# A stack of four gated cross-attention and FFN layers on one core: the first Mamba preparation kept on chip, and input weights kept for a layer's products

## The chip, the cores and the metric

The kernel is one program on one core of a Trainium2 chip. Its time is the device time of one execution in microseconds (us); where several executions were timed, the median stands. Engines: PE multiplies matrices (PEld loads its stationary operand), DVE, ACT and POOL work on tiles of 128 partitions, and SP issues most DMA transfers. ACT issues some too.

## The reference, cut to what matters

Four layers, each a gated cross-attention block and a gated FFN, act on x of shape (4, 512, 512), with a context ctx of shape (4, 512, 256):

```python
x = x + tanh(g_xattn[0]) * L0_xattn(ctx, layernorm(x), ...)   # Mamba
x = x + tanh(g_ffn[0])   * L0_ffn(layernorm(x), ...)          # gated, 2 of 4 kept
x = x + tanh(g_xattn[1]) * L1_xattn(layernorm(x), ctx, ...)   # attention over channels
x = x + tanh(g_ffn[1])   * L1_ffn(layernorm(x), ...)          # ternary weights
x = x + tanh(g_xattn[2]) * L2_xattn(ctx, layernorm(x), ...)   # Mamba
x = x + tanh(g_ffn[2])   * L2_ffn(layernorm(x), ...)          # fp8 weights
x = x + tanh(g_xattn[3]) * L3_xattn(layernorm(x), ctx, ...)   # 16-head attention
x = x + tanh(g_ffn[3])   * L3_ffn(layernorm(x), ...)          # quantised both sides
```

The Mamba blocks are what the change touches. Their recurrence depends on ctx alone; z, made of x, only multiplies its result:

```python
x = einsum('bld,ed->bel', ctx, in_proj_w)
u = silu(conv1d(x, conv_w, width 4, causal) + conv_b)
dt_low, B, C = split(einsum('bdl,ed->bel', u, x_proj_w))      # 16, 16 and 16 rows
dt = softplus(einsum('brl,dr->bdl', dt_low, dt_proj_w) + dt_proj_b)
state = state * exp(dt * A) + (dt * u) * B                    # for each of 512 times
y = sum over 16 states of state * C
y = (y + D * u) * silu(z)
```

## The kernel before, in words

A batch is a "head" (l, b): l is 0 for the first Mamba block and 1 for the second, b one of four batches. The heads run in the order (0,0), (0,1), (1,0), (0,2), (1,1), (0,3), (1,2), (1,3). An l = 0 head goes through Mamba, l0f (the first FFN), l1attn and l1x, and l1f; an l = 1 head through Mamba, l2f and l3x; the last FFN, l3f, comes behind.

For each head the Mamba work has three parts. `mamba_in` (L462) multiplies ctx with the input weights: 4 tiles of 128 channels by 512 times, each from 2 x 3 products, since operands are split into a high and a low part. `mamba_pre` (L486) makes u (convolution L500, tanh L504, L505), the product xd with B, C and dt's low rows (L529), the product dtp (L546 for the first head, L566 for others), softplus through a polynomial log1p (ACT squares L483, DVE steps L484), and from dt also du = dt * u and y = D * u. The scan does 64 steps, 16 states by 4 channel tiles. A step (`state`, L599) is an exp on ACT (L602), a product with B on POOL (L603), the scan on DVE (L605) and a product with C (L606); the sum over states is on POOL (L624), or for the first head on PE (L644).

The first head's three parts, the prologue, run ahead of everything in the pool `pp`; its preparation keeps u, dt, du and y in SBUF (`if pp`). Among its scan steps the loop at the end of the kernel calls `mamba_in` for the seven other heads, whose results go to DRAM (dxin). Their preparations and scans are side work (lists `pres` and `side`): generators that `tick` draws on between the pieces of the main path, the first preparation at once in the first l0f tile (`finish(whole)`). They pass everything through DRAM: u, dtp (ddtp), dt and du (dst) and y (dy) are written and read again, by `copy` (SP queue, L254) and `keep` (ACT queue, L259). B and C go to DRAM as dbc, and each state's two rows are loaded as a bc tile broadcast to all partitions (L596).

`unit` (L266) loads a weight or ctx: at its first use raw, then split on ACT (high part, L263) and on DVE or POOL (low part, L264) and written to DRAM; later uses load the split form (L278). All l0f and l1f weights pass this way in the first head.

The main path needs a scan's end in `xmamba`: the stored y is loaded, multiplied with silu(z) (L663, L665), transposed on PE (xm, L669) and added to x (L671). For the next l = 0 head this is called inside the present block's last `down`.

A scheduler fixes each engine's order when the program is built. It lists the instructions by priority, which is program order; `tick` raises the number for side work, `copy` for its transfers (by 200 in the first block, 60 later), so that these stand behind. At run time each engine and each DMA queue works in its fixed order. Tiles come from pools with a number of buffers per tag, and an instruction that takes a buffer waits for the last reader of the one before.

Of the kernel before, what the change touches and what calls it, by code (L numbers as in the profile page):

```python
# [10 lines left out]
F32 = mybir.dt.float32  # L11
# [9 lines left out]
ADD, SUB, MUL = ALU.add, ALU.subtract, ALU.mult  # L21

B, S, D, CD = 4, 512, 512, 256
# [53 lines left out]
def tile_flamingo(ctx: ExitStack, tc: tile.TileContext, I, out):  # L77
    nc = tc.nc
    v, s, g, pe, sy = nc.vector, nc.scalar, nc.gpsimd, nc.tensor, nc.sync
# [58 lines left out]
    side, pres, prep = [], [], []  # L138
# [73 lines left out]
    for l in range(2):  # L212
        o = l * PAR_MW
        a = cp.tile([128, 64], F32, name=f"nA{l}")
# [3 lines left out]
        c = cp.tile([128, 20], F32, name=f"cw{l}")  # L218
# [24 lines left out]
    scr = {}  # L243
    turn = {"split": 0, "w": 0}

    def dram(key, shape, dt):
        t = dr.tile(shape, dt, name=nm("d" + key), tag=nm("d"))
        return t

    def copy(dst, src):  # L250

        behind = COPIES if phase[0] > 0 else COPIES_FIRST
        tc.cur_priority += behind
        sy.dma_start(dst, src)  # L254
        tc.cur_priority -= behind

    def keep(dst, src):

        s.dma_start(dst, src)  # L259
# [3 lines left out]
        s.copy(dst[:, 0], src)  # L263
        (lo_eng or v).tensor_tensor(dst[:, 1], src, dst[:, 0], op=SUB)  # L264

    def unit(kind, i, cols=512, p=None, tag="w"):  # L266

        t = T(p or wp, [128, 2, cols], FR, tag)
        key = (kind, i)
        if key not in scr:  # L270
            raw = T(wrp, [128, 512], F32, "wr")
            sy.dma_start(raw[:, :cols], I[kind][i])
            turn["split"] += 1
            split(t, raw[:, :cols], lo_eng=g if turn["split"] % 2 or phase[0] < 0 else v)
            scr[key] = dram(kind, [128, 2 * cols], F32)
            copy(scr[key], t.rearrange("p a c -> p (a c)").bitcast(F32))
        else:
            sy.dma_start(t.rearrange("p a c -> p (a c)").bitcast(F32), scr[key])  # L278
        return t
# [177 lines left out]

    xin = {}

    def mamba_in(l, b, stay=None):  # L460

        cu = [unit("ctxT", 2 * b + k) for k in range(2)]  # L462
        iw = [unit(f"M{l}_in", k) for k in range(2)]
        for d in range(4):
            ps = stay() if stay else mmps("in")
            c = slice(d * 128, d * 128 + 128)
            for k in range(2):
                mm3(ps, iw[k][:, 0, c], iw[k][:, 1, c], cu[k][:, 0], cu[k][:, 1], k == 0, k == 1)
# [14 lines left out]
            s.activation(q, t, AF.Square, bias=lpb[:, i : i + 1])  # L483
            v.scalar_tensor_tensor(ac, q, LP[i][1], t if i == 0 else ac, op0=ADD, op1=MUL)  # L484

    def mamba_pre(l, b, mp, pp=None):  # L486

        M = lambda tag, shape=(128, 512), dt=F32: T(mp, list(shape), dt, tag)
        po = l * PAR_MW
        ud = []  # L490
# [31 lines left out]
        for d in range(4):  # L522
# [5 lines left out]
            c = slice(d * 80, d * 80 + 80)  # L528
# [7 lines left out]
        bcd = dram("bc", [32, 512], F32)  # L536
# [27 lines left out]
        for d in range(4):  # L564
            ps = mbps("dtp")
            pe.matmul(ps, dw[:80, 0, d * 128 : d * 128 + 128], st[:80], start=True, stop=True)  # L566
            x = M("mt")
            s.activation(x, ps, AF.Identity, bias=dtb(d))
            keep(tmp[:, d], x)
        yield 1.0  # L570
        for d in range(4):
            dt = M("mt")
            copy(dt, tmp[:, d])
            t = M("mt")
            s.activation(t, dt, AF.Abs)
            s.activation(t, t, AF.Exp, scale=-1.0)
            s.activation(dt, dt, AF.Relu)
            ac = M("mt")
            log1p(t, ac, mbps)
            v.scalar_tensor_tensor(dt, ac, LP_K, dt, op0=MUL, op1=ADD)  # L580
            r = [dram("st", [128, 512], F32) for i in range(2)]
            copy(r[0], dt)
            u = M("mt")
            copy(u, ud[d])
            g.tensor_tensor(dt, dt, u, op=MUL)
            copy(r[1], dt)
            g.tensor_scalar(u, u, Dc(d), 0.0, op0=MUL, op1=ADD)
            copy(ysc[l, b][d], u)
            sc.append(r)
            yield 3.4  # L590
        mst[l, b] = bcd, sc

    def bc_tile(bcd, n, p, bufs, queue=sy):

        bc = p.tile([128, 2, 512], F32, tag="bc", name=nm("bc"), bufs=bufs)
        queue.dma_start(bc, bcd.rearrange("(c n) l -> n c l", c=2)[n].partition_broadcast(128))  # L596
        return bc

    def state(l, b, n, d, dt, du, bc, db, last=v):  # L599
# [8 lines left out]
    def mamba_scan(l, b, mp, red):  # L608

        M = lambda tag: T(mp, [128, 512], F32, tag)  # L610
        bcd, sc = mst[l, b]
        dts, us, ys = [], [], []
        for d in range(4):
            for tag, r, src in (("dt", dts, sc[d][0]), ("du", us, sc[d][1]), ("y", ys, ysc[l, b][d])):
                x = M(tag)
                copy(x, src)
                r.append(x)
        ahead = bc_tile(bcd, 0, mp, mbufs["bc"])
        for n in range(NST):
# [785 lines left out]
    mctx = ExitStack()  # L1405
    wrp = mctx.enter_context(tc.tile_pool(name="wr", bufs=4))
    mp = mctx.enter_context(tc.tile_pool(name="m", bufs=4))
    mbufs = {"bc": 2, "mt": 4, "db": 3, "fc": 2, "fw": 2, "kn": 4, "fv": 4, "sq": 1}
    _T = T

    def T(p, shape, dt, tag, name=None):
# [33 lines left out]
    heads = [Head(*h) for h in ((0, 0), (0, 1), (1, 0), (0, 2), (1, 1), (0, 3), (1, 2), (1, 3))]  # L1445
    with psum(mb=2, y=4), tc.tile_pool(name="pro", bufs=1) as pp:
        z4 = lambda: pp.tile([128, 512], F32, tag="z", name=nm("z"), bufs=8)
        mamba_in(0, 0, lambda: bank("y", "in"))
        list(mamba_pre(0, 0, mp, pp))
        scan = mamba_scan_pe(0, 0, pp)  # L1450
        for i, _ in enumerate(scan):
            if i % 7 == 6 and i < 49:
                h = heads[i // 7 + 1]
                mamba_in(h.l, h.b)
            if i == 32:
                heads[0].load(z4, z4)
        for h in heads[1:]:
            side.append(((h.l, h.b), mamba_scan(h.l, h.b, mp, on_g)))
            pres.append(((h.l, h.b, "pre"), mamba_pre(h.l, h.b, mp)))
        xmamba(0, 0, heads[0].xs, heads[0].zs, None, mbps)  # L1460
        heads[0].turn(mbps)
    side.append((("w3",), l3f_prep(mp)))
# [113 lines left out]
```

## Time and profile before

| What | us |
|---|---|
| Median of 3 timed runs | 3509.45 |
| Lowest, highest | 3498.4, 3509.68 |
| The profiled execution | 3500.79 |
| Its span, first to last instruction | 3499.0 |
| PE busy in the span | 3063.6 (88%) |
| DVE busy | 2536.3 (72%) |
| ACT busy | 1988.9 (57%) |
| POOL busy | 1728.6 (49%) |
| Moved by DMA | 720.95 MB, 206 GB/s in the mean |

Milestones of the profiled execution, from the rows of the tiles named:

| Milestone | from, us | to, us |
|---|---|---|
| scan of head (0,0) (L605, db00x) | 59.6 | 193.1 |
| its x update (L671) | 199 | 203 |
| first l0f, gate and up (L700 to L703) | 223 | 341 |
| dtp product of head (0,1) (L566) | 255 | 261 |
| scan of head (0,1) (db01x) | 358.2 | 619.3 |
| l1f of head (0,0), gate and up | 465 | 535 |
| l1f of head (0,0), down (L416) | 549 | 589 |
| x update of head (0,1) | 637 | 641 |
| second l0f, gate and up | 657 | 796 |
| scan of head (1,0) (db10x) | 670.6 | 976.8 |
| scan of head (0,2) (db02x) | 1013.7 | 1270.4 |

Read it so: busy shares over the whole span mix stages with different limits. A stage is read from its own stretch, by who is busy in it and what the others wait for. The granted clock of PE was 0.946 in the mean.

### The profile page before, as it was taken

To read this page: it belongs to the slowest core of one execution; us is meant where nothing else is said; L and a number is where in the kernel's file an instruction comes from. 1 tells how busy PE (TensorE), PEld (TensorE's weight loads), DVE (VectorE), ACT (ScalarE), POOL (GpSimd) and SP (SyncE) were. 2 spreads that over 40 slices of the span, in tenths; PEclk is the share of its full clock that TensorE was granted. 3 is DMA by queue.
4 is the path that set the end of the run, shared out by engine and by line. 5 is a ranking of instruction groups with operands and counts; after the bars stand their busy time and mean duration, and the time that the engine had idled before them with its cause. 6 is when DMAs were issued, how large, how long until landed. Compare 5 with 4: busy or idle time off the path is not lost.

```text
span 3499.0 us, 41084 instructions
## 1 busy us (share of the span) xinstructions
PE 3063.6 (88%) x12460; PEld 1994.9 (57%) x12474; DVE 2536.3 (72%) x4160; ACT 1988.9 (57%) x4405; POOL 1728.6 (49%) x1369
## 2 busy tenths in 40 slices
PE   6779986588898889888998899899998999989996
PEld 4347463464666555475575555475766555666663
DVE  6867897899779789889688799975335445655454
ACT  6437474454654777654564577553534767656673
POOL 5823795347667578556576689820101313213121
PEclk8889998799999899999999899999999999999998
DMA  8649577875685565485677554397755444466551
GB/s 308 211 169 357 196 264 269 309 250 186 229 275 176 205 195 143 132 298 186 203 260 240 178 169 159 93 340 258 247 194 186 133 121 157 151 211 206 177 157 46
DMA packets 323070, 720.95 MB, mean 206 GB/s; under 512 B 33025, under 2 KB 34433, under 8 KB 322849
## 3 DMA queue, kind: packets, MB, share of 16 engines
q1 hardware_dynamic: 269008, 617.65, 51.7%
q10 hardware_dynamic: 53840, 100.68, 10.1%
q8 instruction: 99, 1.62, 0.2%
q14 instruction: 123, 1.00, 0.1%
HBM read 553.25 MB, written 164.95 MB: 205 GB/s over the span
## 4 chain that ended last, share of the span: by engine, by line
PE 38%; DVE 24%; ACT 9%; DMA 9%; issue 8%; POOL 7%; SPq 0%; ACTq 0%; DVEq 0%; POOLq 0%
DVE mb L605 7%; PE acc L416 3%; POOL y L624 3%; PE S L833 3%; PE down L1029 2%; PE gate L700 2%; PE gate L701 2%; PE up L700 2%; PE up L701 2%; PE l L1373 2%; PE po L1011 2%; ACT P L840 1%; PE down L1163 1%; PE pT L848 1%; PE acc L895 1%
## 5 line engine op out<-in xcount | busy, mean ns | idle before, releaser
L602 ACT ACTIVATE mb<-dt,nA 128x512 f32<-128x512 f32 x512 | 352.3, 692 | 452.4 <-DVE db10x L606 64.6
L340 POOL TENSOR_TENSOR sm<-sm,mhalf 128x4 f32<-128x4 f32 (+4 forms) x104 | 143.5, 1380 | 516.2 <-DVE sm L370 233.8
L700 PE MATMUL gate<-xT,w 128*128 128x512 f32 x624 | 257.9, 413 | 46.1 <-DVE xT L264 20.1
L833 PE MATMUL S<-k,q 128*128 128x512 f32 x512 | 263.1, 626 | 28.8 <-ACT P L840 23.7
L700 PE MATMUL up<-xT,w 128*128 128x512 f32 x624 | 246.8, 396 | 8.5 <-DVE hf L753 5.5
L701 PE MATMUL gate<-xT,w 128*128 128x512 f32 x624 | 250.6, 402 | 0.0
L416 PE MATMUL acc<-w,hf 128*128 128x512 f32 x512 | 229.5, 604 | 22.6 <-DVE hf L728 17.1
L834 DVE TENSOR_REDUCE st<-S 128x1 f32<-128x512 f32 x256 | 173.4, 682 | 99.3 <-PE S L833 98.6
L701 PE MATMUL up<-xT,w 128*128 128x512 f32 x624 | 244.8, 392 | 0.0
L340 POOL TENSOR_TENSOR sml<-sml,mhalf 128x1 f32<-128x1 f32 x32 | 17.8, 558 | 418.7 <-DVE sml L370 223.5
L840 ACT ACTIVATE P<-S,st,sm 128x512 f32<-128x512 f32 x256 | 199.5, 784 | 39.3 <-DVE st L838 28.9
L1011 PE MATMUL po<-pt,v 128*128 128x512 f32 x384 | 203.9, 614 | 19.6 <-ACT pt L850 19.6
L848 PEld LDWEIGHTS pT<-ident,P 128*128 128x128 f32 x1024 | 127.3, 144 | 128.7 <-issue 56.8
L850 ACT COPY pt<-pT 128x512 f32<-128x512 f32 x256 | 148.8, 590 | 77.7 <-PE pT L848 75.4
L848 PE MATMUL pT<-ident,P 128*128 128x128 f32 x1024 | 164.7, 281 | 29.6 <-ACT P L840 12.1
L416 PEld LDWEIGHTS acc<-w,hf 128*128 128x128 f32 x512 | 97.7, 193 | 146.1 <-issue 112.9
L703 PE MATMUL gate<-xT,w 128*128 128x512 f32 x432 | 172.7, 400 | 0.0
L1029 PE MATMUL down<-wo,h 128*128 128x512 f32 x384 | 170.7, 593 | 0.0
L703 PE MATMUL up<-xT,w 128*128 128x512 f32 x432 | 169.7, 393 | 0.0
L700 PEld LDWEIGHTS gate<-xT,w 128*128 128x128 f32 x624 | 121.4, 195 | 81.7 <-DVE xT L264 21.6
L343 PE MATMUL Q<-w,xT 128*128 128x256 f32 x512 | 159.4, 312 | 7.3 <-ACT xT L263 5.2
L416 PE MATMUL acc<-w,h 128*128 128x512 f32 x352 | 154.0, 594 | 0.0
(314 smaller groups left out, 9110.0 us busy)
## 6 DMA issues: line engine op xcount, KB each, us to landing
bc<-dbc ACTq DMA_DIRECT2D x105, 512.0 KB, 5.5
w<-dL_g SPq DMA_DIRECT2D x81, 512.0 KB, 5.3
w<-dL_u SPq DMA_DIRECT2D x81, 512.0 KB, 5.1
w<-in_L_d_dram SPq DMA_DIRECT2D x68, 512.0 KB, 5.8
w<-dL_q SPq DMA_DIRECT2D x64, 512.0 KB, 5.0
w<-dL_gu SPq DMA_DIRECT2D x48, 512.0 KB, 5.1
v<-dv SPq DMA_DIRECT2D x80, 256.0 KB, 5.6
k<-dk SPq DMA_DIRECT2D x80, 256.0 KB, 3.6
```

What stands on the lines that cost most here:

```text
L416: pe.matmul(ps, h[:, c], w, start=first, stop=last)
L602: s.activation(ps, dt, AF.Exp, scale=nA[l][:, d * 16 + n : d * 16 + n + 1])
L605: v.tensor_tensor_scan(h, ps, db, 0.0, MUL, ADD)
L700: pe.matmul(ps, wh[:, c], xT[k][:, 0], start=k == 0, stop=False)
L701: pe.matmul(ps, wh[:, c], xT[k][:, 1], start=False, stop=wl is None and k == 3)
L703: pe.matmul(ps, wl[:, c], xT[k][:, 0], start=False, stop=k == 3)
L833: pe.matmul(ps, q[:, c], k[t * len(k) // NT], start=True, stop=True)
L834: v.tensor_reduce(st[:, t : t + 1], ps, AX.X, ALU.max, negate=True)
L840: s.activation(p, ps, AF.Exp, scale=r, bias=m, accum_out=st[:, 8 + t : 9 + t])
L848: pe.transpose(ps[:, t * 128 : t * 128 + 128], pt[t][:, kt * 128 : kt * 128 + 128], ident)
L1011: pe.matmul(po, vs[kt][:, c], u, start=kt == 0, stop=kt == 3)
L1029: pe.matmul(ps, hs[j][:, c], ws[j // 2][:, j % 2], start=j == 0, stop=j == 3)
```

## The change

Four things are changed.

1. `unit` takes `again`; with `again=False` a first use isn't written to DRAM. The input weights of a layer are loaded and split once, into the tag "iw" (2 buffers) of the prologue's pool, and kept in `inw` for the layer's four products, instead of being stored and loaded again for each head.
2. The seven `mamba_in` calls among the scan's steps go by layer and batch, (0,1), (0,2), (0,3), (1,0) to (1,3), instead of in the order of the heads.
3. Everything that they issue on SP stands behind the issue of the fourth bc tile (`rows[3]`): `tc.issue_after` orders instructions of the same engine, without a semaphore.
4. The preparation of head (0,1), the first that runs beside the main path, is called with `here=True`: dtp goes straight into the dt tile, log1p and softplus work on it there, u is loaded from DRAM into the du tile, y and du are made there, and `mamba_scan` takes the three tiles of each d as they are. The first three reloads of u for xd and the dxin and u transfers stay.

```diff
-    def unit(kind, i, cols=512, p=None, tag="w"):
+    def unit(kind, i, cols=512, p=None, tag="w", again=True):
...
-            scr[key] = dram(kind, [128, 2 * cols], F32)
-            copy(scr[key], t.rearrange("p a c -> p (a c)").bitcast(F32))
+            if again:
+                scr[key] = dram(kind, [128, 2 * cols], F32)
+                copy(scr[key], t.rearrange("p a c -> p (a c)").bitcast(F32))
...
-    def mamba_in(l, b, stay=None):
+    def mamba_in(l, b, pp, stay=None):
...
-        iw = [unit(f"M{l}_in", k) for k in range(2)]
+        if l not in inw:
+            inw[l] = [unit(f"M{l}_in", k, p=pp, tag="iw", again=False) for k in range(2)]
+        iw = inw[l]
...
-            x = M("mt")
+            x = M("dt" if here else "mt")
             s.activation(x, ps, AF.Identity, bias=dtb(d))
-            keep(tmp[:, d], x)
+            if here:
+                sc.append([x])
+            else:
+                keep(tmp[:, d], x)
...
-            dt = M("mt")
-            copy(dt, tmp[:, d])
+            if here:
+                dt = sc[d][0]
+            else:
+                dt = M("mt")
+                copy(dt, tmp[:, d])
...
+            if here:
+                du, y = M("du"), M("y")
+                sy.dma_start(du, ud[d])
+                g.tensor_scalar(y, du, Dc(d), 0.0, op0=MUL, op1=ADD)
+                g.tensor_tensor(du, dt, du, op=MUL)
+                sc[d] += [du, y]
+                yield 3.4
+                continue
...
-        queue.dma_start(bc, bcd.rearrange("(c n) l -> n c l", c=2)[n].partition_broadcast(128))
+        i = queue.dma_start(bc, bcd.rearrange("(c n) l -> n c l", c=2)[n].partition_broadcast(128))
+        rows.append(i.ins)
...
-        dts, us, ys = [], [], []
-        for d in range(4):
+        dts, us, ys = zip(*sc) if len(sc[0]) == 3 else ([], [], [])
+        for d in range(4 - len(dts)):
...
-        mamba_in(0, 0, lambda: bank("y", "in"))
+        mamba_in(0, 0, pp, lambda: bank("y", "in"))
...
-                h = heads[i // 7 + 1]
-                mamba_in(h.l, h.b)
+                with tc.issue_after(rows[3]):
+                    mamba_in(*divmod(i // 7 + 1, B), pp)
...
-            pres.append(((h.l, h.b, "pre"), mamba_pre(h.l, h.b, mp)))
+            pres.append(((h.l, h.b, "pre"), mamba_pre(h.l, h.b, mp, here=h is heads[1])))
```

More of the change, by code (lines that the diff above doesn't have):

```diff
@@ L458, in tile_flamingo @@
     xin = {}
-    def mamba_in(l, b, stay=None):
+    inw = {}
+    def mamba_in(l, b, pp, stay=None):
         cu = [unit("ctxT", 2 * b + k) for k in range(2)]
-        iw = [unit(f"M{l}_in", k) for k in range(2)]
+        if l not in inw:
+            inw[l] = [unit(f"M{l}_in", k, p=pp, tag="iw", again=False) for k in range(2)]
+        iw = inw[l]
         for d in range(4):
@@ L484, in log1p, with mamba_pre @@
             v.scalar_tensor_tensor(ac, q, LP[i][1], t if i == 0 else ac, op0=ADD, op1=MUL)
-    def mamba_pre(l, b, mp, pp=None):
+    def mamba_pre(l, b, mp, pp=None, here=False):
         M = lambda tag, shape=(128, 512), dt=F32: T(mp, list(shape), dt, tag)
@@ L591, in mamba_pre @@
         mst[l, b] = bcd, sc
+    rows = []
     def bc_tile(bcd, n, p, bufs, queue=sy):
         bc = p.tile([128, 2, 512], F32, tag="bc", name=nm("bc"), bufs=bufs)
-        queue.dma_start(bc, bcd.rearrange("(c n) l -> n c l", c=2)[n].partition_broadcast(128))
+        i = queue.dma_start(bc, bcd.rearrange("(c n) l -> n c l", c=2)[n].partition_broadcast(128))
+        rows.append(i.ins)
         return bc
@@ L1407, in tile_flamingo @@
     mp = mctx.enter_context(tc.tile_pool(name="m", bufs=4))
-    mbufs = {"bc": 2, "mt": 4, "db": 3, "fc": 2, "fw": 2, "kn": 4, "fv": 4, "sq": 1}
+    mbufs = {"iw": 2, "bc": 2, "mt": 4, "db": 3, "fc": 2, "fw": 2, "kn": 4, "fv": 4, "sq": 1}
     _T = T
```

## The prediction, made before the changed kernel had run

> **What bounds the kernel now.** I read the page's slices first, then the busy time by stretch, then who waited for whom, and last the rows of the tiles that the change touches.
>
> The slices (87.5 us each; PE, DMA):
>
> ```profile
> PE   6779986588898889888998899899998999989996
> ...
> DMA  8649577875685565485677554397755444466551
> ```
>
> PE is near its limit except in the prologue (slices 1 to 3), in slices 7 and 8 (525 to 700 us) and in the last. The stretches, with the busy time of PE, PEld, DVE, ACT and POOL in each, then clock, DMA share and GB/s:
>
> ```profile
> 204.00:223.00 19.00, 5.73 (x17) 3.38 (x18) 12.55 (x22) 9.53 (x16) 1.90 (x3) 0.50 0.35 111
> 223.00:358.00 135.00, 132.64 (x551) 101.34 (x550) 98.16 (x160) 91.84 (x225) 37.67 (x26) 0.99 0.95 346
> 358.00:590.00 232.00, 206.68 (x690) 125.51 (x690) 190.91 (x253) 128.41 (x276) 178.71 (x137) 0.94 0.68 229
> 590.00:637.00 47.00, 4.28 (x16) 2.86 (x16) 40.77 (x54) 18.53 (x30) 25.54 (x19) 0.52 0.92 320
> 637.00:670.00 33.00, 22.21 (x91) 16.39 (x92) 25.71 (x51) 18.37 (x32) 6.68 (x6) 0.81 0.90 298
> 670.00:800.00 130.00, 113.85 (x466) 88.79 (x465) 129.64 (x180) 67.29 (x158) 64.52 (x43) 0.93 0.77 267
> ```
>
> From 590 to 637 us PE has 4.3 us of work in 47. From 670 to 800 DVE is the bound (129.6 of 130). The waits between 358 and 660 us name what PE stood for (total, times, longest):
>
> ```profile
> PE xm L669 <- DVE z L663: 43.7, 4, 37.2
> ```
>
> The xm transposes need z times y, and y is the scan of head (0,1). The scan's own rows (min, median, max in ns, then first and last start):
>
> ```profile
> L605 DVE TENSOR_TENSOR_SCAN mb<-mb,db00x x48: 1205/1222/1232, 59.6 to 186.1; 128x512 f32<-128x512 f32 x48
> ...
> L605 DVE TENSOR_TENSOR_SCAN mb<-mb,db01x x64: 1191/1222/1232, 358.2 to 618.1; 128x512 f32<-128x512 f32 x64
> ```
>
> So scan (0,1) runs late because it starts only at 358 us, when the 16 gate/up tiles of the first l0f are done, though the preparation's last product (dtp) ended at 261 us. In between lie the round trips through DRAM:
>
> ```profile
> L254 SPq DMA_DIRECT2D mt<-ddtp x4: 319/320/1036, 262.0 to 319.5; - x4
> ...
> L254 SPq DMA_DIRECT2D dst<-mt x8: 319/319/944, 278.9 to 369.2; - x8
> L254 SPq DMA_DIRECT2D dt<-dst x4: 320/409/995, 282.6 to 360.7; - x4
> L254 SPq DMA_DIRECT2D du<-dst x4: 320/454/755, 289.3 to 371.2; - x4
> ```
>
> They stand in one SP queue with weights that take 0.95 of the DMA engines, and the last du is issued at 371 us.
>
> **The change part by part.**
>
> *Preparation of (0,1) on chip.* It removes 32 transfers of 256 KB: 4 ddtp out (ACT queue) and 4 in, 8 dst out, 4 dt and 4 du in, 4 y out and 4 in (SP); the 4 reloads of u become 4 loads of du. 28 x 0.26 MB + the 4 on ACT = 8.4 MB, some 24 us of the 346 GB/s of that stretch. That buys no time by itself: PE was busy 132.6 of 135 there. POOL's eight operations (du, y) stay, in other tiles. No buffer is waited for: the prologue's scan frees dt, du and y by 193 us.
>
> What it moves I read from the two kernels as built, engine by engine. In DVE's order, counted from the x update of head (0,0) at 204 us: the first scan step of (0,1) stood behind 16 finished hf tiles and stands behind 10, whose tenth ended at 305 us before. Ahead of the last mask of this l0f stand 223 instructions instead of 186: 15 L605, 15 L606, 6 L500, 1 L505 more: 15 x 1.22 + 15 x 0.69 + 6 x 0.74 + 0.69 = 33.8 us. DVE idled 135 - 98.2 = 36.8 us in that stretch. So the work just fits into the hole, and I take 33.8 us as what the scan gains. Bounds: nothing, if the in-order steps delay the hf tiles and PE with them; at most 43.7 us, since PE waits no longer than that for the scan. Once that wait is gone, the last two l1f down rows, the layer norm and the four lnT products (20 us from x to the first gate) are late next; they were late before too.
>
> Ahead of the x update of (0,1) DVE has 463 instructions instead of 491: 10 L297, 9 L301, 10 L302, 2 L450 and 2 L451 less, 4 L484 and 1 L580 more (10 x 0.42 + 9 x 0.69 + 10 x 0.68 + 4 x 0.69 - 5 x 0.68 = 16.6 us less). That is fp8 preparation for the third block, and it only moves behind that update, into a stretch where DVE has no idle time: counted as zero, given back by the end of that l0f. From DVE's 1298th instruction (1133 us) to the 3134th (2700 us) both orders are equal, so what is gained by then is carried.
>
> *DVE beside POOL.* The scan's POOL operations now run beside l0f's masks and splits. The rows of 223 to 640 us:
>
> ```profile
> L715 DVE TENSOR_TENSOR cm<-ha,ha x24: 678/693/1797, 241.5 to 348.7; 128x512 bf16<-128x512 f32 x24
> ...
> L264 DVE TENSOR_TENSOR w<-wr,w x24: 673/692/1832, 230.2 to 535.7; 128x512 fp32r<-128x512 f32 x24
> ```
>
> Some of them take 1.1 us longer than the median. Between the scan's first step and the last mask stand 51 such instructions (12 L715, 11 each of L726, L727, L728, 6 L264). Taken from L264 between 358 and 590 us, where POOL is 77% busy and the median is 0.81 us for w and 1.07 for fw instead of 0.69, the mean stretch is about 0.2 us: 51 x 0.2 = 10 us lost. Bounds: 0 and 51 x 1.1 = 56 us.
>
> The Trainium skill (SBUF, section "Who interferes with whom") says that a VectorE instruction with both inputs in SBUF and a GpSimd one that reads SBUF exclude each other, so that the second to issue waits for the whole of the first. This speaks against the change, and the maxima above agree with it, the medians say that most are not hit. By the rule at its worst, each of the 51 behind a whole 1.28 us POOL operation, the sum would end 65 - 10 = 55 us later than mine.
>
> *The input weights.* 4 stores and 12 reloads of dM_in (512 KB each) go, 8.4 MB; PE waited 17.9 us for them, but only one wait reached the scan: step 1 at 59.6, step 2 at 66.4 us, since ACT's copy of a product stood in between. These 6.8 us are the most that can be gained.
>
> *ctx behind the first rows of B and C.* On SP the loads of ctx for heads (0,1) on are now queued behind the four bc loads, which before landed at 43.1, 47.9, 49.4 and 51.8 us. On ACT, six splits of ctx (0.6 us each) and two copies now stand among the log1p squares (L483) that lead to dt, where two copies stood; ahead of the first square four copies and three splits are gone, 4.2 us, of which I count 3, since the dtp product sets its start too. So in-order ACT reaches the first split at about 46 us (first square at 43.0 - 3, then nine operations of 0.65 us) and waits for ctx until 51.8 + 0.65 = 52.5 us. Behind it wait ten L483, for them DVE's L484, and for those every scan step: 6 us of wait and 4.8 of work come in, 1.2 and 3 go, and the first step would come at 59.6 + 6.6 = 66 us, the second right after it, where it came at 66.4 before. Bounds: -6.8 (no wait) to +6 (twice the wait); I take 0. From there DVE's pace of 1.93 us per step is unchanged. POOL gets five splits between the first du and the last; 5 x 1.3 us, inside the same wait.
>
> *Late.* The l3f side work is dealt a little differently and ACT loads its tables 6 times more (16 to 19 at L1320, 15 to 18 at L840), 1.283 us each: 0 to 7.7 us while PE is 0.95 busy; I take 3.
>
> **Sum.** -33.8 + 10 + 0 + 3 = -20.8. The profiled execution took 3500.79 us (span 3499.0 and 1.8 around it): 3480. The median of the three runs is 3509.45, 8.7 above that execution, the lowest 3498.4; against the median it is -0.84%.
>
> **Rivals.**
> *The whole wait goes.* PE's 43.7 us and the 6.8 of the prologue are won, nothing is lost: 3500.8 - 50.5 = 3450. For it: the DVE idle time of 223 to 637 us sums to 84 us, more than is needed. Against: POOL is 77% busy in the scan's stretch, and DVE is full after 670.
> *Hidden anyway.* The scan starts earlier but its steps are dealt among hf, masks and splits, and PE's l0f loses what the x update wins: 3500.8 + 3 - 0 to 10, about 3498. For it: PE was 98% busy in 223 to 358, so each late hf costs PE time. Against: the scan took 261 us for 64 steps, 4.1 us a step, where DVE needs 1.9 and POOL 2.6.
> *Slower.* The stretching of DVE beside POOL in the first l0f: at the maximum 51 x 1.1 = 56 us, and all 7.7 us of tables: -33.8 + 56.1 + 7.7 = +30, 3531. It decides from 0.6 us mean stretch on (30.8 / 51). For it: both maxima. Against: medians of 0.81 and 1.07 beside a POOL at 77%.
>
> **How the numbers follow.** The forecast has 0.5 (3480, alone 3465 to 3495), the whole wait 0.15, hidden anyway 0.2, slower 0.15. The range runs from 3450 to 3512: it takes in the whole wait and the hidden case and leaves out most of the stretched one. 0.5%, 17.5 us of the median, is about what this measurement can tell from no change: under 3492 lie nearly all of the forecast's 0.5, 0.15 and a little of the hidden case (0.63 after taking off the forecast's upper edge), over 3527 lie 0.13, the upper part of the slower case, and 0.24 between.
>
> **What would show it.** Right: the first L605 of db01x near 305 us instead of 358, the wait of xm for z under 15 us instead of 43.7, the first gate of the second l0f near 630 instead of 657, and L715 and L726 with medians hardly raised. Wrong: db01x first seen after 340; a first db00x scan step later than 75 us with ACT waiting for wr; the last hf of the first l0f past 375 instead of 345 us; or a second l0f that takes back more than it was given.

## The result, and the profile after

| | before | changed |
|---|---|---|
| median, us (12 runs each) | 3501.5 | 3515.58 |
| lowest to highest | 3496.61 to 3509.68 | 3503.91 to 3520.97 |
| span of the profiled execution | 3499.0 | 3512.1 |

The change makes the kernel 0.37% slower (ratio 1.0037, 95% interval 1.0026 to 1.0048). The forecast was 3480 us. Over the 12 runs the kernel before has a median 8 us under that of the three runs in the first table.

The page of the changed kernel, its slices of 87.5 us:

```profile
PE   6868978788798889988998899899998999989995
...
DMA  6548469875685564385587554397655435466541
```

Slices 7 and 8 went from 6 and 5 tenths to 8 and 7: the gap is partly filled. But 3, 4, 6, 11 and the last lost a tenth each. To see where the gain went I cut both kernels at the ends of the same five instructions: the x update of (0,0), the last mask (L728 before, L752 after) of the first l0f, the x update of (0,1), the last mask of the second l0f, and the x update of (1,0). An x update has four rows; at (0,1) the cut is at the first of them, at the others at the last. Columns as in the prediction: the stretch and its length, busy time and count of PE, PEld, DVE, ACT and POOL, granted clock, DMA share, GB/s. Before:

```profile
202.70:358.30 155.60, 138.67 (x568) 104.91 (x569) 112.28 (x187) 101.67 (x242) 39.81 (x29) 0.92 0.87 315
358.30:637.30 279.00, 210.84 (x705) 128.19 (x705) 231.68 (x306) 146.66 (x304) 204.25 (x155) 0.87 0.72 244
637.30:840.70 203.40, 166.56 (x626) 119.04 (x627) 195.72 (x282) 102.99 (x237) 93.24 (x63) 0.92 0.75 254
840.70:1008.60 167.90, 154.63 (x587) 104.00 (x591) 121.43 (x179) 99.04 (x228) 111.00 (x89) 0.97 0.76 251
```

After, the same four stretches:

```profile
204.10:394.30 190.20, 159.01 (x593) 113.69 (x594) 160.43 (x224) 113.62 (x263) 88.14 (x62) 0.88 0.69 235
394.30:617.80 223.50, 190.10 (x652) 120.58 (x653) 180.85 (x242) 127.92 (x276) 162.12 (x123) 0.90 0.74 249
617.80:846.70 228.90, 181.92 (x668) 123.98 (x669) 221.32 (x304) 111.05 (x250) 118.16 (x81) 0.92 0.71 249
846.70:1027.00 180.30, 158.60 (x574) 105.83 (x574) 131.91 (x196) 101.81 (x229) 96.62 (x74) 0.90 0.75 262
```

Read the lengths first: +34.6, -55.5, +25.5, +12.4. The change did win what it was to win, but in the second stretch alone, and paid it back in the three others: +17.0 in all. Then PE: stretch minus busy is its idle time, 16.9 + 68.2 + 36.8 + 13.3 = 135.2 us before, and 31.2 + 33.4 + 47.0 + 21.7 = 133.3 after. The one long wait for the scan has turned into many short ones of the same sum, and for the same number of products (2486 and 2487) PE was busy 18.9 us longer (the last section shows in which products). Behind the x update of (1,0) 4 us come back; from the 1103rd DVE instruction behind the first cut (1132.5 and 1146.9 us) to the end it is 2363.7 us before and 2362.4 after. With 1.4 us more in the prologue the span is 13.1 us longer.

The scans moved as intended. After, and before for the third head:

```profile
L629 DVE TENSOR_TENSOR_SCAN mb<-mb,db01x x64: 1190/1219/1232, 308.7 to 591.1; 128x512 f32<-128x512 f32 x64
L629 DVE TENSOR_TENSOR_SCAN mb<-mb,db10x x64: 1196/1218/1232, 639.1 to 971.5; 128x512 f32<-128x512 f32 x64
```

```profile
L605 DVE TENSOR_TENSOR_SCAN mb<-mb,db10x x64: 1198/1219/1232, 670.6 to 975.6; 128x512 f32<-128x512 f32 x64
```

(0,1) starts 50 us earlier and ends 27 earlier. (1,0), which nobody had touched, starts 31 us earlier too, and ends only 4 earlier. Ahead of the last mask of the second l0f now stand 36 steps of it instead of 28: 8 x 1.9 = 15 us of DVE work in a stretch where DVE had no idle time.

The two-operand masks of the first l0f beside POOL, DVE's time for 16 L727 and 16 L728 before (same stretch as above):

```profile
202.70:358.30 155.60, 7.45 (x16) 0.92 0.87 315
...
202.70:358.30 155.60, 10.68 (x16) 0.92 0.87 315
```

and for the same lines after, L751 and L752:

```profile
204.10:394.30 190.20, 11.64 (x16) 0.88 0.69 235
...
204.10:394.30 190.20, 13.83 (x16) 0.88 0.69 235
```

0.47 us each became 0.73, and 0.67 became 0.86. Over the 1103 DVE instructions behind the x update of (0,0), which are the same in both kernels line by line, the sum of durations rose from 844.9 to 875.5 us. I call lengthening what each of them takes over the shortest quarter of its line in the kernel before: 78 us before, 110 after. DVE's idle time (elapsed time less all durations) fell from 85 to 67. So an idle gain of 18 us was paid with 31 us of lengthening: +13. This account of DVE and the one of PE above describe the same loss and aren't to be added.

And PE's waits from 795 to 1085 us, after (total, times, longest):

```profile
PE gate L724 <- DVE xT L264: 13.7, 2, 10.0
PE acc L418 <- DVE hf L752: 13.3, 5, 5.3
PE dtp L573 <- DMA mt<-ddtw: 8.9, 1, 8.9
```

The third wait is new: before, the dt weights landed at 887.8 us, ahead of need; now SP issues them only at 891.4, behind the end of the fp8 preparation.

### The profile page after: what moved, and what is told of

The parts are those of the page before. It is cut to its first block, busy times and chain, and to the rows that moved or that the text cites. A ratio compares the mean times of both kernels' runs of the same rounds, so it can differ in the third digit from the quotient of the medians.

```text
span 3512.1 us, 40977 instructions
## 1 busy us (share of the span) xinstructions
PE 3084.2 (88%) x12461; PEld 2002.2 (57%) x12474; DVE 2563.3 (73%) x4160; ACT 1994.1 (57%) x4411; POOL 1739.5 (50%) x1369
## 4 chain that ended last, share of the span: by engine, by line
PE 36%; DVE 23%; issue 8%; ACT 8%; DMA 8%; POOL 7%; SPq 1%; ACTq 0%; DVEq 0%; POOLq 0%
DVE mb L629 7%; PE S L857 3%; PE acc L418 3%; POOL y L648 3%; PE gate L724 2%; PE gate L725 2%; PE up L724 2%; PE up L725 2%; PE down L1053 2%; PE po L1035 2%; PE l L1397 1%; PE pT L872 1%; PE down L1187 1%; PE gate L727 1%; ACT P L864 1%
## 5 line engine op out<-in xcount | busy, mean ns | idle before, releaser
L724 PE MATMUL gate<-xT,w 128*128 128x512 f32 x624 | 262.1, 420 | 62.3 <-DVE xT L264 35.6
L418 PE MATMUL acc<-w,hf 128*128 128x512 f32 x512 | 239.0, 624 | 35.1 <-DVE hf L752 25.5
L725 PE MATMUL gate<-xT,w 128*128 128x512 f32 x624 | 253.1, 406 | 0.0
L727 PE MATMUL gate<-xT,w 128*128 128x512 f32 x432 | 176.1, 408 | 0.0
L727 PE MATMUL up<-xT,w 128*128 128x512 f32 x432 | 168.6, 390 | 0.0
```

The lines of the kernel that those rows point to most:

```text
L418: pe.matmul(ps, h[:, c], w, start=first, stop=last)
L724: pe.matmul(ps, wh[:, c], xT[k][:, 0], start=k == 0, stop=False)
L725: pe.matmul(ps, wh[:, c], xT[k][:, 1], start=False, stop=wl is None and k == 3)
L727: pe.matmul(ps, wl[:, c], xT[k][:, 0], start=False, stop=k == 3)
```

## The experiments

Two tables hold the readings. The ratios are of timed runs, all else is of one profiled execution each. The marks, in us, are the ends of the stretches above, counted from the x update of (0,0).

| kernel | ratio to before (95%) | last mask 1 | x (0,1) | last mask 2 | x (1,0) | PE busy |
|---|---|---|---|---|---|---|
| before | 1 | 156 | 435 | 638 | 806 | 671 |
| changed | 1.0037 (1.0026, 1.0048) | 190 | 414 | 643 | 823 | 690 |
| changed_again | 1.0031 (1.0019, 1.0043) | 187 | 413 | 643 | 823 | 686 |
| here_alone | 1.0001 (0.9988, 1.0014) | 188 | 411 | 640 | 821 | 682 |
| here_again | 0.9998 (0.9987, 1.0009) | 191 | 413 | 644 | 823 | 686 |
| weights_alone | 0.9959 (0.9947, 0.9971) | 167 | 435 | 640 | 813 | 676 |
| weights_again | 0.9954 (0.9939, 0.9969) | 168 | 432 | 637 | 810 | 675 |
| weights_free | 1.0044 (1.0029, 1.0060) | 159 | 449 | 649 | 820 | 677 |
| no_ddtw | 0.9989 (0.9976, 1.0002) | 185 | 406 | 628 | 815 | 686 |
| ddtw_on_act | 0.9997 (0.9986, 1.0007) | 187 | 412 | 643 | 821 | 686 |
| scan_behind | 1.0009 (0.9995, 1.0023) | 186 | 439 | 648 | 814 | 676 |
| no_sum_before | 0.9834 (0.9819, 0.9850) | 157 | 355 | 577 | 765 | 666 |
| no_sum_after | 0.9838 (0.9816, 0.9860) | 174 | 361 | 585 | 763 | 668 |
| no_fp8_dve_before | 0.9869 (0.9851, 0.9887) | 160 | 426 | 613 | 775 | 668 |
| no_fp8_dve_after | 0.9889 (0.9869, 0.9909) | 187 | 416 | 611 | 784 | 674 |
| fp8_cast_before | 0.9950 (0.9933, 0.9968) | 156 | 435 | 631 | 800 | 670 |
| fp8_cast_after | 0.9976 (0.9966, 0.9986) | 187 | 417 | 645 | 814 | 684 |
| fp8_cast_weights | 0.9956 (0.9941, 0.9972) | 169 | 437 | 629 | 799 | 671 |
| fp8_psum_before | 1.0163 (1.0142, 1.0183) | 160 | 421 | 617 | 796 | 674 |
| fp8_psum_after | 1.0160 (1.0143, 1.0177) | 187 | 410 | 609 | 785 | 675 |

DVE's account over the 1103 instructions (765 to 769 us of shortest work in every row; in weights_free, no_ddtw and scan_behind a handful of them are others), and the rest of the execution, in us:

| kernel | elapsed | lengthening | idle | behind |
|---|---|---|---|---|
| before | 929.8 | 78 | 85 | 2363.7 |
| changed, changed_again | 942.8, 943.3 | 110, 109 | 67, 69 | 2362.4, 2365.5 |
| here_alone, here_again | 939.6, 941.7 | 106, 107 | 68, 69 | 2355.6, 2360.0 |
| weights_alone, weights_again | 933.9, 931.0 | 86, 88 | 82, 76 | 2359.2, 2349.0 |
| weights_free | 942.0 | 82 | 91 | 2365.6 |
| no_ddtw | 936.7 | 100 | 71 | 2361.5 |
| ddtw_on_act | 941.1 | 110 | 65 | 2357.7 |
| scan_behind | 935.2 | 95 | 72 | 2368.6 |

**The halves of the change.** `here_alone` is before with the preparation on chip, `weights_alone` the changed kernel without it; both were run twice.

```diff
+ here=h is heads[1]        # here_alone: this part of the change alone
- here=h is heads[1]        # weights_alone: all but this
+ here=False
```

> The kernel before with the preparation of (0,1) kept on chip, and nothing else of the change. Theory 'VectorE budget' (the preparation moves 33 us of DVE work into the first l0f, where DVE has only some 17 us to spare behind the fourth hf tile, and puts its two-operand instructions beside POOL operations that lengthen them, some 30 us more between 204 and 1130 us than before): this part alone does it all, 10 to 17 us slower than before, with about 130 lengthened DVE instructions between the x update of (0,0) and the 1103rd DVE instruction behind it, against 99. Rival 'prologue' (the loss comes from the input weights or from ctx behind the rows of B and C): this part alone is faster than before, by up to 20 us. Rival 'late ddtw load' and rival 'fp8 moved' expect 10 to 13 us slower too; they are told apart by the other runs.

> The changed kernel with the preparation of (0,1) through DRAM as before: the input weights, the order of the products and ctx behind the rows of B and C stay. VectorE budget: within 4 us of before, since the prologue's scan ended within 1.5 us of before's and DVE's work behind it is the same. Rival 'prologue': 8 to 17 us slower than before.

> The changed kernel itself, beside its two halves on one chip. 'VectorE budget with lengthening': 8 to 16 us slower than before, and in its profile again over 100 us of lengthening and under 70 us of idle time of DVE between the x update of (0,0) and the 1103rd DVE instruction behind it (940 us long, give or take 4). Rival 'chance' (the 13 us are the scatter of single executions and of chips): within 5 us of before.

> The input weights and the ctx order alone, a second time. If their 14 us of gain are real: a ratio between 0.9945 and 0.9975 to before again, 20 us and more ahead of changed_again. If they were chance: 0.999 to 1.001. Budget theory: 930 to 936 us from the x update of (0,0) to the 1103rd DVE instruction, with 80 to 90 us of lengthening and about 82 of idle time, as before the change.

> The preparation of (0,1) on chip alone, a second time. Budget with lengthening: 936 to 943 us to the 1103rd instruction, where the kernel before took 930, with 100 to 110 us of lengthening; and what it gives back must lie elsewhere, behind that instruction, where its order of instructions differs from before's: less than 2360 us there, against 2364. Rival 'the first run was chance': 5 to 13 us slower than before in the median.

In the stretch that the theory speaks of, all five came out as it says: each of them with `here` takes 940 to 943 us with 106 to 110 of lengthening, those without it 931 to 934 with 86 to 88, so that a repeat differs by 3 us at most. In the total they did not: `here` alone costs nothing, the weights alone win 15 and 19 us, and both together lose 10 to 14. The rest lies behind the 1103rd instruction, where no instruction of the change is left, but the scheduler's list is ordered differently: 2356 to 2360 us for `here`, 2349 to 2359 for the weights, 2362 to 2366 for the changed kernel, whose DVE order there is that of before up to the 3134th instruction. These are single executions (that of weights_alone, 3498.65 us, is its slowest), and behind the mark the two of the weights differ by 10 us. So the sign of the total is partly a matter of how the list falls out, by some 10 us; that the loss of the changed kernel is no chance is shown by its second run. Why one order is faster than another there stays open.

**The place of ctx.**

```diff
-                with tc.issue_after(rows[3]):
-                    mamba_in(*divmod(i // 7 + 1, B), pp)
+                mamba_in(*divmod(i // 7 + 1, B), pp)
```

> The input weights kept and the products by layer, without setting ctx behind the rows of B and C and without the preparation on chip. If ctx behind the rows is what gains: no faster than before; if the kept weights (8.4 MB less to move) gain: as fast as weights_again. In the prologue the first scan step comes near 60 us instead of 65, the second near 66 in both. Budget theory: no difference over 5 us from weights_again.

The kept weights alone gain nothing, as the first alternative said: 3518.22 us, against 3485.91 for weights_again and 3504.49 for before on one chip. The budget theory misses by 32 us, though the prologue ends at the same time (202.2 and 202.5 us, last scan step at 193.9 in both); its first step came at 67.7 us, not near 60. Its lengthening is as small as before's (82), its idle time larger (91), and the x update of (0,1) comes 17 us later, behind 505 DVE instructions instead of 482. So lengthening is not the only way to lose 13 us here.

**The late load.**

```diff
-        dw = unit_dtw(l, mp)                                         # no_ddtw
+        dw = unit_dtw(l, mp) if pp else st.rearrange("p (a c) -> p a c", a=1)
...
-            sy.dma_start(t[:80, 0].bitcast(F32), scr[key])           # ddtw_on_act
+            s.dma_start(t[:80, 0].bitcast(F32), scr[key])
```

> The changed kernel without the reload of the dt weights for the heads behind the first: the dtp product takes the tile st for both operands, so dt is not the reference's. Rival 'late ddtw load' (PE stood 8.9 us at the dtp product of (0,2) behind a load that SP issued at 891 us, and the products of l1x stood behind it): 9 to 13 us faster than the changed kernel, so equal to before. VectorE budget: the wait of PE goes, but the time stays within 5 us of the changed kernel, since DVE's work and its lengthening beside POOL are the same.

> The changed kernel with the reload of the dt weights issued on ACT's queue instead of SP's. DVE's order of instructions is the same up to the 1315th and PE's up to the 3017th, so that nothing but the load differs up to 1147 us. Rival 'late ddtw load': PE's wait of 8.9 us at the dtp product of (0,2) goes, the 943 us from the x update of (0,0) to the 1103rd DVE instruction become 930 to 934, and the kernel is 9 to 13 us faster than the changed one. Budget with lengthening: 938 to 944 us there and within 5 us of the changed kernel up to that point, whether PE waits or not.

`no_ddtw` ends 14.6 us under changed_again, a little more than the rival said, but not where it said: the wait is gone, and the stretch from the last mask to the x update of (1,0), in which it lay, grew from 180 to 187 us, since the lnT transposes took over (14.7 us of wait in place of 3.7). What it wins lies earlier, in an order that had changed as well, with 10 us less lengthening. `ddtw_on_act` kept the orders, but only moved the wait to another queue:

```profile
PE dtp L573 <- DMA mt<-ddtw: 7.6, 1, 7.6
```

Its 941.1 us up to the 1103rd instruction are the changed kernel's within the scatter, although the wait is 1.3 us shorter; most of the 12 us by which it is faster than changed_again lie behind, in another order. So the late load looks like a symptom worth at most a few us here; no run removes it with all orders kept.

**The displaced fp8 work.**

```diff
-            behind = 0 if q is pres and r == 1.0 else 500 if q is prep or not phase[0] else BEHIND
+            behind = 0 if q is pres and r == 1.0 else 500 if q is prep else BEHIND
```

> The changed kernel with the side work of the first block set back by 1000 instead of 500 in the scheduler's list. In the order built from it DVE has 493 instructions between the x updates of (0,0) and (0,1), as before the change (496; the changed kernel has 466): the fp8 preparation stays ahead of the second update. Rival 'fp8 moved' (16.6 us of fp8 work pushed into the full second l0f give the gain back): the time falls by the 16 us to about 3499. VectorE budget: where this work stands doesn't matter once DVE is full, so within 5 us of the changed kernel, with the lengthening as large (100 us and more to the 1103rd instruction).

3510.27 us: by the medians 4 to 5 under the changed kernel, by the ratios to before on the same chip 8 to 10, with some 6 of uncertainty. That is less than the 16 of the rival and, by the ratios, more than the 5 of the budget theory. The fp8 work stands ahead of the x update of (0,1) again, and that update comes at 439 instead of 414 us: the whole gain is gone there, and the second l0f takes 209 us again instead of 229. That x (1,0) comes 9 us earlier than in the changed kernel fits neither theory alone; lengthening is down to 95 us.

**Less POOL.** The sums over the states are left out for two heads, in both kernels.

```diff
+                if (l, b) not in ((0, 1), (1, 0)):
                     red(d).tensor_tensor(ys[d], ys[d], db, op=ADD)
```

> The kernel before without the sums over the states on POOL for the heads (0,1) and (1,0): 128 POOL additions of 1.28 us less, y there is D * u alone. 'VectorE budget with lengthening' (a DVE instruction with both operands in SBUF that is issued while a POOL instruction runs takes up to 1.1 us longer): of the 78 us by which DVE instructions are lengthened between the x update of (0,0) and the 1103rd DVE instruction behind it, a third goes, to about 50, and the time falls by 15 to 30 us. Rival 'the loss is queueing, not lengthening' (late loads and in-order waits; the lengthening happens where DVE would wait anyway): less than 10 us faster than before.

> The changed kernel without the same 128 POOL additions. Budget with lengthening: the lengthening falls from 110 to about 70 us, so by more than in the kernel before, and the changed kernel's loss of 13 us against it shrinks to between -5 and +5 us over the stretch to the 1103rd instruction. Rival 'queueing': the changed kernel stays 10 to 15 us behind no_sum_before.

From the x update of (0,0) to that of (1,0): before, changed, no_sum_before, no_sum_after.

```profile
202.70:1008.60 805.90, 670.70 (x2485) 456.13 (x2492) 661.11 (x949) 450.35 (x1009) 448.29 (x335) 0.91 0.76 262
```

```profile
204.10:1027.00 822.90, 689.63 (x2484) 464.08 (x2490) 694.51 (x961) 454.39 (x1016) 465.05 (x339) 0.90 0.72 249
```

```profile
198.20:963.70 765.50, 665.98 (x2482) 453.54 (x2488) 642.75 (x949) 447.68 (x1006) 281.58 (x206) 0.93 0.80 274
```

```profile
201.70:964.90 763.20, 668.30 (x2482) 453.79 (x2488) 637.90 (x955) 450.84 (x1012) 288.36 (x210) 0.93 0.77 268
```

As it was put, the rival 'queueing' falls. POOL's busy time (the fifth pair) fell from 448 and 465 us to 282 and 288, and with that the two kernels are equal, 3444.79 and 3446.13 us; up to the 1103rd instruction the change now wins 13 us (893.9 to 880.5) where it had lost 13, more than I expected, with 64 and 53 us of lengthening (I had expected 50 and 70) and equal idle time of DVE (62, 61). The gain of 57 us is twice what I expected: idle time fell as well, not lengthening alone. The pair doesn't isolate the lengthening: without the additions the scan of (0,1) itself ends earlier (its x update comes 80 and 53 us earlier), and DVE's order is another one, with 424 and 451 instructions between the x updates of (0,0) and (0,1) instead of 496 and 466 (to the last row). What it shows is that with less POOL work the loss is gone.

**The same instructions with an operand in PSUM.**

```diff
-        s.activation(raw, raw, AF.Copy, scale=2.0**-20)
+        ps = mbps("f8")
+        s.activation(ps, raw, AF.Copy, scale=2.0**-20)
-        v.scalar_tensor_tensor(raw, m, 1.5 * 2.0**-6, raw, op0=ALU.max, op1=ADD)
-        v.scalar_tensor_tensor(raw, m, 1.5 * 2.0**-6, raw, op0=ALU.max, op1=SUB)
+        v.scalar_tensor_tensor(ps, m, 1.5 * 2.0**-6, ps, op0=ALU.max, op1=ADD)
+        v.scalar_tensor_tensor(raw, m, 1.5 * 2.0**-6, ps, op0=ALU.max, op1=SUB)
```

> The kernel before with one edit: the fp8 preparation's scaled copy lies in a PSUM bank, so that the add and the subtract of the rounding have one operand in PSUM. Lengthening theory: these 72 instructions, of which 27 are lengthened by about 1 us each before, run at 0.68 to 0.75 us at the longest, about 20 us less of lengthening. In the order built, 17 of the 36 preparations' instructions move behind the x update of (1,0), since the bank is shared with the scans: the time falls by 5 to 20 us if this is hidden, and rises by up to 20 if the third block waits for its weights. Rival (the long instructions are long for another reason, such as a wait for their input): the same share stays above 1 us.

> The changed kernel with the same edit. Lengthening theory: 21 lengthened instructions of the rounding go, about 20 us; the masks beside the scan stay lengthened, so some 10 to 20 us of the 31 us more than in fp8_psum_before remain, and it ends 0 to 15 us behind fp8_psum_before. Rival as above: the same share stays above 1 us.

The two instructions before, and in fp8_psum_before (min, median, max in ns):

```profile
L301 DVE SCALAR_TENSOR_TENSOR wr<-wr,wr x36: 668/693/1775, 556.2 to 815.9; 128x512 f32<-128x512 f32 x36
...
L302 DVE SCALAR_TENSOR_TENSOR wr<-wr,wr x36: 664/680/1783, 558.5 to 820.4; 128x512 f32<-128x512 f32 x36
```

```profile
L302 DVE SCALAR_TENSOR_TENSOR f<-wr,f x36: 664/685/697, 806.7 to 1189.7; 128x512 f32<-128x512 f32 x36
...
L303 DVE SCALAR_TENSOR_TENSOR wr<-wr,f x36: 668/677/687, 808.1 to 1190.8; 128x512 f32<-128x512 f32 x36
```

Not one of 72 is lengthened. They run later than before, but not for that beside an idle POOL: 48 of the 72 began while a POOL instruction ran (before, 34, of which 27 were lengthened). The first instruction of the same preparation, which the edit left as it was, still is lengthened in fp8_psum_before, in 14 of the 21 cases that began beside POOL:

```profile
L297 DVE TENSOR_SCALAR wr<-wr x36: 398/430/1483, 551.5 to 1184.1; 128x512 int32<-128x512 int32 x36
```

The time rose by 57 us all the same, more than expected: sharing the bank with the scans, the preparation ran from 807 to 1190 us, and the third block waited for its weights. Up to the x update of (1,0), ahead of most of that work, fp8_psum_after leads by 11 us (785 against 796). In the end the two are level (3561.6 and 3558.22 us), where I had expected fp8_psum_after up to 15 us behind.

**Less DVE in the second l0f.** First by a cast to fp8 and back on ACT, then by leaving the three instructions out.

```diff
-        m = T(wrp, [128, 512], F32, "wr")                            # fp8_cast
+        m = T(wrp, [128, 512], F8, "wr")
+        s.copy(m, raw, saturate=True)
+        s.activation(raw, m, AF.Copy, scale=-(2.0**-20))
-        s.activation(raw, raw, AF.Copy, scale=2.0**-20)              # fp8_cast
-        v.tensor_scalar(...)                                         # both
-        v.scalar_tensor_tensor(...)
-        v.scalar_tensor_tensor(...)
```

> The kernel before, with the fp8 preparation's three DVE instructions replaced by a cast to fp8 and back on ACT (72 ACT instructions of 0.6 us where 36 stood, 108 DVE instructions less: 63 us at their shortest, 87 with their lengthening). Budget: DVE is what is short between 590 and 860 us, so the time falls by 45 to 80 us. Rival 'PE and its waits set the time': less than 20 us, since PE's work is the same.

> The changed kernel with the same cast. Budget: with DVE no longer full in the second l0f, the 20 us that the change had won at the x update of (0,1) are no longer given back there: faster than fp8_cast_before by 5 to 20 us at the x update of (1,0), and 0 to 15 us in the end. Rival (the loss has nothing to do with DVE's time in the second l0f): again 10 to 15 us behind fp8_cast_before.

> The kernel of weights_alone with the same cast: the version that may beat both kernels. Budget: 45 to 80 us faster than weights_alone, 3410 to 3445 us. Rival: less than 20 us faster.

13 us, not 45 to 80, fp8_cast_weights no faster than weights_alone (3489.54 us), and the change still loses, 14 us at x (1,0) and 6 in the median. Groups of ACT in fp8_cast_before, of the cast and of the scan's exp behind it (busy us, mean ns):

```profile
L297 ACT ACT_TABLE_LOAD x25 | 32.1, 1283 | 2.4 <-DMA wr<-in_L_u_dram 1.9
...
L598 ACT ACT_TABLE_LOAD x13 | 16.7, 1283 | 0.6 <-ACT mt L564 0.4
```

82 loads instead of 32: ACT took DVE's place (192 us busy of 600 to 860, where it was 125). These runs don't tell, so the instructions were left out instead:

> The kernel before without the three DVE instructions of the fp8 preparation (ACT's scaling and all transfers stay; the weights of the third block are then not rounded to fp8). 63 us of DVE work at its shortest go, 87 with its lengthening, between 548 and 820 us, and nothing is added elsewhere. Budget (DVE's time is what is short there): 25 to 60 us faster than before; PE's own work, some 175 us of the 200 in the second l0f, bounds it. Rival 'not DVE': less than 10 us faster.

> The changed kernel without the same 108 DVE instructions. Budget: the 20 us that the change had won at the x update of (0,1) survive the second l0f, so it reaches the x update of (1,0) 5 to 20 us ahead of no_fp8_dve_before, and ends 0 to 20 us ahead. Rival 'not DVE' (PE's and ACT's in-order waits give the gain back in the second l0f whatever DVE has to do): again 10 to 16 us behind no_fp8_dve_before at the x update of (1,0) and in the end.

45 us less: DVE's time is what is short there. But the 10 us won at the x update of (0,1) (426 to 416) are 2 at the last mask and -9 at x (1,0), a miss: I had expected them to survive. Without the fp8 work the loss is halved (9 of 17 us, 7 of 13 in the median), no more.

## Why the prediction was wrong, step by step

- *The scan starts near 305 us, no wait of xm.* Right: 308.7; the list of PE's waits from 358 to 660 us has no xm any more. But the second l0f's first gate came at 647 us, where I had said 630.
- *33.8 us fit into DVE's 36.8 us of idle time, and the scan gains them.* This step failed first. Of the idle time of that stretch 20 us lay ahead of the fourth mask, at 273 us, and the scan comes at 309; from there on DVE had 9.8 us before, and 0.1 are left after. The moved work and its lengthening pushed the last mask from 358 to 394 us and PE's idle time there from 17 to 31. The x update of (0,1) still came 19.5 us earlier, because the first l0f's end was not what it waited for. A hole must be read from where the moved work can start, not from the stage's sum.
- *DVE beside POOL, +10.* The mechanism was right, the size was not: the 51 instructions that I had counted were lengthened by 22 us in all, 0.44 each and not 0.2. I had read the 0.2 from medians. The means of the same rows, 358 to 590 us before, lie 0.38 us over 0.69, which gives 19 us:

```profile
L264 DVE TENSOR_TENSOR w<-wr,w 128x512 fp32r<-128x512 f32 x11 | 11.3, 1029 | 3.7 <-ACT w L263 3.7
...
L264 DVE TENSOR_TENSOR fw<-wr,fw 128x512 fp32r<-128x512 f32 x4 | 4.7, 1169 | 0.0
```

  Of the 31 us over the 1103 instructions 19 lie ahead of the last mask of the first l0f (12 to 31, 14 instructions to 34 with more than 0.15 us); of what I had not counted, the second l0f has 9. My sign, medians of L715 and L726 hardly raised, failed too: in the first l0f that of L726 stayed (415 ns), that of L715 (L739 after) went from 693 to 923:

```profile
L739 DVE TENSOR_TENSOR cm<-ha,ha x24: 672/923/1796, 245.1 to 377.7; 128x512 bf16<-128x512 f32 x24
```

- *fp8 preparation counted as zero, given back by the end of that l0f.* It contradicts the sum, which carried the full gain on. Only 3 of its displaced triples ended up ahead of the second l0f's last mask, 7 behind it; and what I had not asked is who else gets ready earlier: 8 steps of scan (1,0). Together 20 us in a full stretch, which took 229 us instead of 203.
- *Input weights and ctx, 0.* Right for the prologue: first step at 65.1, second at 66.2 us, end +1.4. That weights_alone is 15 to 19 us faster, I had no step for.
- *Late part, +3.* ACT has its 6 more table loads, and all that lies behind the 1103rd instruction is the same within 2 us; what the loads cost alone no run shows.
- *Equal orders from the 1298th instruction on carry the difference.* Right: 2363.7 and 2362.4 us. They carried a loss.
- *A step that was missing.* Of SP's queue behind 855 us I had followed nothing: 8.9 us of PE's wait.
- *The rivals.* What came was two of them in one: 'hidden anyway' (PE's first l0f loses what the x update wins), and a part of 'slower', by more lengthening than the 10 us. I had priced them apart, each on its own.

What is shown: the time goes in the stretches above; the lengthening comes with the preparation on chip, and vanishes with an operand in PSUM; without the POOL additions the loss vanishes; PE's longer products lie where its granted clock was 0.5 (last section). What is argued only: that the waits for lengthened and reordered DVE work bring that clock on. What stays open: the share of each in the 13 us, since no run holds one of them fixed, and the order's part behind 1147 us. Of the versions that leave nothing out weights_alone is the fastest: 3490.28 and 3485.91 us, 0.9959 (0.9947 to 0.9971) and 0.9954 (0.9939 to 0.9969) of before, and 29 us under the changed kernel on one chip.

## What to carry to other kernels

Work that becomes ready earlier is also issued earlier, by engines that work in order: before counting a removed wait as won, list what will now stand ahead of the critical instructions, in this stage and, for the next producer of the same kind, in the following one. Idle time counts only from where the moved work can start, and beside POOL a DVE instruction that other rows show lengthened is to be priced by its mean in a stretch as crowded as the new one, not by its median. Where a list scheduler orders the program, an edit's own effect is read from marks with equal work between them, since the total carries some 10 us of reordering elsewhere.

## What the runs showed of the hardware

- Of the lengthening of DVE 76 of the 78 us before and 108 of the 110 after lie in instructions that began while a POOL instruction ran; of the others none was lengthened by more than 0.04 us. The Trainium skill (SBUF, section "Who interferes with whom") says that a VectorE instruction with at most one SBUF input, outside the 2-port modes, doesn't contend with GpSimd; the rounding with one operand in PSUM, 697 ns at the longest where it was 1783, agrees. One operand alone is no safeguard here: L297 reads one tile in SBUF, and its 427 ns became up to 1498 in the kernel before. Which mode it ran in no row shows. The prediction's worst case, a whole POOL operation of 1.28 us, was nearly met: 1.2 us were the most in the two kernels.
- PE's short waits cost more than themselves. The first 128 products of l0f's down, before and after (PE, PEld, clock, DMA share, GB/s):

```profile
345.00:420.00 75.00, 55.74 (x128) 24.30 (x128) 0.94 0.58 196
```

```profile
361.00:440.00 79.00, 60.60 (x128) 25.64 (x128) 0.94 0.40 122
```

  A product takes 0.592 us in the median. Before, none of the 128 is longer; after, 15 are, ten of them with 0.957 to 1.222 us, and nine of these ten ran wholly at a granted clock of 0.5. Over the whole stretch between the x updates of (0,0) and (1,0), what products took over the median of their line (lines with 20 products or more, over 0.05 us) sums to 50.0 us before and 67.6 after; 33.4 and 50.9 of it lie in products at a granted clock of 0.5. That is the difference in PE's busy time but for a us or two. Within the stretch, which begins at one half, the clock fell to it 12 times before and 19 times after, and stood there for 140 and 164 us in all. Before each fall PE had been busy for at most half of the 3.4 us ahead, with 1.5 to 4.6 us for the longest wait in the 6.8 us ahead. The Trainium skill (TensorE: Matmul & The Clock Gate, section "Part 1: The HAM clock gate (the "warmup" mystery)") has a clock of one half after an idle window of some 3.4 us; the ratio of 1.222 to 0.592 agrees with the half, but here shorter waits were enough. No run here varies the waits alone.
- ACT's cast to fp8 and back brought 50 table loads of 1283 ns that the scaling by Copy had not, some of them in the scan's exp that follows.
